# Last attention of a four-part transformer block: turned weights in two PSUM banks, ScalarE sharing their copy, pieces in the single bank, and the output bias as a row of the projection

## The chip, the cores and the metric

The kernel runs on one core of a Trainium2 chip. Its metric is the device time in microseconds of one execution; lower is better. Everything is float32. Beside the plain time of several runs there is one execution taken by the hardware profiler: each engine's instructions with start and duration. PE is the matrix engine (TensorE), DVE is VectorE, ACT is ScalarE, POOL is GpSimd, SP starts transfers. "PEclk" is the clock that the matrix engine was granted, 1.0 being full speed. PSUM, where matmuls write, has eight banks of 512 float32 values per partition here: `ps_s` holds three buffers of two banks, `ps_mm` is one bank, `ps_o` is one bank.

## The reference, cut to what matters

x has 8 sequences of 512 rows of 256 values. Four residual blocks follow one another: attention a, a feedforward block of two layers, attention b, and the same feedforward block again. The change touches attention b alone (16 heads of 16 values):

```
x = x + attn_a(layernorm(x)); x = x + ffn(layernorm(x))
x = x + attn_b(layernorm(x)); x = x + ffn(layernorm(x))
# attn_b
q, k, v   = split(x @ w_qkv + b_qkv, 3), by heads
dot       = einsum('bhid,bhjd->bhij', q, k)
scores    = dot*dot / (|q|^2 + |k|^2.T - 2.0*dot + 1e-6) + causal mask
out       = softmax(scores) @ v
return out @ w_out + b_out
```

## The kernel before, in words

The 8 sequences are taken in two groups of 4. For each group the program runs attention a, a feedforward block, attention b and a feedforward block, so there are two attention b stages, each over 4 sequences ("batches" in the code).

**A unit.** Attention b is cut into units: one block of 128 query rows, the key blocks up to the diagonal, and two or more heads. Row block 0 has 2 units of 8 heads x 128 keys, row block 1 has 4 units of 4 heads x 256, row block 2 has 8 units of 2 x 384, row block 3 has 8 units of 2 x 512. That is 22 units for a batch and 88 for a stage; all are 128 x 1024 in size, but those of row block 2, which are 128 x 768. For a unit, in the order of its data:

- PE computes the denominator (`den`) and the dot products (`dot`), each into a two-bank buffer of `ps_s` (L1079).
- ACT forms 1/den as exp(-ln(den)) (`inverse`, two instructions of L228); DVE repairs it by one Newton step: `error` (L1098, which reads `den` in PSUM) and `refine` (L1102).
- ACT squares `dot` into SBUF (`squares`, L1108); POOL adds the causal mask on the diagonal block (L1110).
- DVE multiplies by 1/den and takes the row maximum (`highest`, one instruction and one accumulator read a head, L1118); ACT takes the exponentials with their row sums (`exponentials`, L228, one a head).
- PE transposes the weights in 128 x 128 blocks (`turn`, L1148) and DVE copies them to SBUF (`keep_turned`, L1153). Before the change, the unit's two halves, 4 transposes each (3 in row block 2), go one after the other through the single bank `ps_mm`: transposes, copy, transposes, copy.
- PE multiplies them with the values into `ps_o` (`values`).

**A step.** The order of the work is written out by hand: `each_part(s)` issues a different stage of several units, one unit a step. Step s issues, on PE: `den` of unit s interleaved with `dot` of s-1, first half of `turn` of s-3, the first part of a piece, in odd steps the `values` of units s-5 and s-4, then the second half of `turn`, and the second part of the piece; on DVE: `refine` of s-1, `highest` of s-2, first `keep_turned`, `error` of s, second `keep_turned`, and the DVE part of a piece; on ACT: `inverse` of s, the ACT part of a piece, `squares` of s-1, `exponentials` of s-2. A helper (`order_keeper`) ties every instruction to the one issued before it on its engine, so this order is the order of execution. The engines themselves wait only for data and for buffers.

**Pieces.** In each step at most one "piece" of other work rides along. Projections of a finished row block are two pieces: `turned`, four transposes of the inverse sums (L1191), an ACT copy (L1195) and a DVE multiply (L1199); and `projected`, four matmuls (L1204) and the DVE addition to x (L1209). The prologue of the next batch is eleven: one that turns the normalized rows (8 transposes, L967, one ACT copy of 128x1024, L971); eight "side" pieces (`project` two matmuls L981, ACT square L991, the norm matmuls L994, DVE `keep_side` L1007), which are not placed in the steps with `values`; and two value pieces (matmuls L1024, DVE addition L1038). Before the change each of these takes one of the three buffers of `ps_s`. What is left of a prologue when its batch starts (each 22 steps) is run whole, piece after piece, with no other work in between.

**Norms.** Ahead of a prologue the rows of the next batch are normalized in the first two steps of the batch before it: statistics on DVE (and 1/std on POOL, L250 and L251), then the rows on DVE, and with them POOL adds the output bias to x in place (L953).

The steps of the prediction are to be followed in `each_part`, the loop under it, and the functions printed here:

Of the kernel before, what the change touches and what calls it, by code (L numbers as in the profile page):

```python
# [17 lines left out]
P = 128  # L18
# [26 lines left out]
def kernel(  # L45
# [152 lines left out]
    keep(near[:, 1, :], -1, NEG)  # L198
    causal = const.tile([P, P], F32, name="causal")
# [740 lines left out]
    def attention_b(batches, g):  # L940
        wl_b, wr_b, wv_b, wo_b, bv_b, bo_b = weights_b(g)

        def normalized(b):
# [6 lines left out]
            def rows():  # L950
                yr = pool.tile([P, NT, D], F32, tag="yr", name=f"yr_b{b}", bufs=1)
                normalize_rows([xs[b]], [yr], got["mv"], got["rstd"])
                nc.gpsimd.tensor_add(xs[b], xs[b], bo_b.unsqueeze(1).to_broadcast([P, NT, D]))  # L953
                state[b] = {"yr": yr}
# [3 lines left out]
        def stacks_and_values(b):  # L958
# [4 lines left out]
            def turned():  # L963
                got["pt"] = ps_s.tile([P, 2, NT, P], F32, tag="s", name=f"pyt_b{b}")
                for k in range(2):
                    for t in range(NT):
                        nc.tensor.transpose(got["pt"][:, k, t, :], state[b]["yr"][:, t, k * P : (k + 1) * P], ident)  # L967

            def columns():
                got["yT"] = pool.tile([P, 2, T], F32, tag="hT", name=f"yT_b{b}")  # L970
                nc.scalar.copy(got["yT"], got.pop("pt").rearrange("p k t c -> p k (t c)"))  # L971

            yield Piece(False, first=turned, act=columns)

            def side_piece(side, w, j):
                vec = vec_b[:, side, j, :]

                def project():
                    got["pu"] = ps_s.tile([P, 2, T], F32, tag="s", name=f"pu_b{b}_{side}_{j}")[:, 0]
# [38 lines left out]
            def value_piece(t2):  # L1018
                def project():
                    got["pv"] = ps_s.tile([P, 2, 2, HB * HDB], F32, tag="s", name=f"pv_b{b}_{t2}")  # L1020
                    for i in range(2):
                        t = 2 * t2 + i
                        for k in range(2):
                            nc.tensor.matmul(  # L1024
                                got["pv"][:, i, 0],
# [6 lines left out]
                def keep_values():  # L1032
# [4 lines left out]
                    for i in range(2):  # L1037
                        nc.vector.tensor_add(state[b]["v"][:, 2 * t2 + i, : HB * HDB], pv[:, i, 0], bv_b)  # L1038
# [21 lines left out]
        def unit(b, i, qp, js, first, last):  # L1060
# [84 lines left out]
            def turn(p, a):  # L1145
                ppt = ps_mm.tile([P, NT, P], F32, tag="mm", name=f"ppt_{n}_{a}")
                for k in range(cols // P):
                    nc.tensor.transpose(ppt[:, k, :], p[:, a, k * P : (k + 1) * P], ident)  # L1148
                return ppt

            def keep_turned(ppt, pt, a):
                nblocks = cols // P
                nc.vector.tensor_copy(pt[:, a, :nblocks, :], ppt[:, :nblocks, :])  # L1153
# [24 lines left out]
            def project(sums):  # L1178
# [9 lines left out]
                def turned():  # L1188
                    got["prt"] = ps_s.tile([P, 2, 4, P], F32, tag="s", name=f"prt_{n}")[:, 0]
# [11 lines left out]
                def projected():  # L1201
                    got["pp"] = ps_s.tile([P, 2, T], F32, tag="s", name=f"pp_{n}")[:, 0, :D]
                    for k in range(4):
                        nc.tensor.matmul(  # L1204
                            got["pp"], lhsT=got["oT"][:, k, :], rhs=wo_b[:, k, :], start=(k == 0), stop=(k == 3)
# [17 lines left out]
        def run(ahead):  # L1223
# [3 lines left out]

            tables_of(EXP_TABLES)
            each, count = len(units) // len(batches), len(units)
            den, dot, r, t, num, most, sums, ppt, pt = ({} for _ in range(9))  # L1230
# [16 lines left out]
            def each_part(s):  # L1247
# [24 lines left out]
                if unit_of(3):  # L1272
                    pt[s - 3] = pool.tile([P, 2, NT, P], F32, tag="pt", name=f"pt_{units[s - 3].n}", bufs=3)
                    turned = units[s - 3].turn(num[s - 3], 0)
# [7 lines left out]
                do(piece.act)  # L1282
                if unit_of(1):
                    num[s - 1] = units[s - 1].squares(dot.pop(s - 1))
                if unit_of(2):
                    most[s - 2] = units[s - 2].highest(num[s - 2], r.pop(s - 2))
                if unit_of(3):
                    units[s - 3].keep_turned(turned, pt[s - 3], 0)
                    turned = units[s - 3].turn(num.pop(s - 3), 1)
                do(piece.second)  # L1290
                if unit_of(2):
                    sums[s - 2] = units[s - 2].exponentials(num[s - 2], most.pop(s - 2))
                if unit_of(0):
                    t[s] = units[s].error(den.pop(s), r[s])
                if unit_of(3):
                    units[s - 3].keep_turned(turned, pt[s - 3], 1)
# [141 lines left out]
```

## Time and profile before

| what | us |
|---|---|
| three runs, median | 4909.79 |
| their lowest and highest | 4900.09 and 4925.63 |
| the profiled execution | 4923.95 |
| its span in the profile | 4922.2 |
| busy in the span: PE, DVE, ACT, POOL | 4458.2, 3161.6, 2244.1, 1276.0 |
| mean granted clock of PE | 0.945 |
| first attention b stage, about 1133 to 1697 | some 564 |
| second attention b stage, about 3584 to 4150 | some 566 |

The two stages are about 23% of the span; the change has no instruction in the rest. In each of them DVE is busy for 87% of the time and PE for 78%, at a mean clock of 0.79 to 0.87 in its parts, while over the whole span PE is busy for 91% and DVE for 64%. A group of instructions in the profile is one line of the kernel, one engine, one operation and one shape, with its busy time and the mean of one in ns; a wait is the idle time of an engine ahead of an instruction, with what ended it.

### The profile page before, as it was taken

To read this page: it belongs to the slowest core of one execution; us is meant where nothing else is said; L and a number is where in the kernel's file an instruction comes from. 1 tells how busy PE (TensorE), PEld (TensorE's weight loads), DVE (VectorE), ACT (ScalarE), POOL (GpSimd) and SP (SyncE) were. 2 spreads that over 40 slices of the span, in tenths; PEclk is the share of its full clock that TensorE was granted. 3 is DMA by queue.
4 is the path that set the end of the run, shared out by engine and by line. 5 is a ranking of instruction groups with operands and counts; after the bars stand their busy time and mean duration, and the time that the engine had idled before them with its cause. 6 is when DMAs were issued, how large, how long until landed. Compare 5 with 4: busy or idle time off the path is not lost. (4 is left out here: it accounts for less than half of the span.)

```text
span 4922.2 us, 68727 instructions
## 1 busy us (share of the span) xinstructions
PE 4458.2 (91%) x26240; PEld 2701.7 (55%) x26240; DVE 3161.6 (64%) x7400; ACT 2244.1 (46%) x5228; POOL 1276.0 (26%) x1164
## 2 busy tenths in 40 slices
PE   8999899898778898998999998998987778989989
PEld 5666556554444465565566665565544444655655
DVE  5667537627988776276356684376289987753762
ACT  3345325416777653154133452253177775532541
POOL 0024214312222243143100242142122222421431
PEclk9999899998888899999999998999988888999999
DMA  2000000000000000000100000000000000000000
GB/s 74 1 20 5 22 18 4 18 6 18 1 1 1 18 5 6 3 18 14 45 27 1 18 5 22 18 5 22 0 18 1 1 1 18 5 5 18 5 6 17
DMA packets 50922, 63.17 MB, mean 13 GB/s; under 512 B 6257, under 2 KB 45345, under 8 KB 50593
## 3 DMA queue, kind: packets, MB, share of 16 engines
q1 hardware_dynamic: 50592, 58.77, 3.7%
q8 instruction: 208, 3.41, 0.3%
q14 instruction: 122, 0.99, 0.1%
HBM read 46.19 MB, written 4.19 MB: 10 GB/s over the span
## 5 line engine op out<-in xcount | busy, mean ns | idle before, releaser
L1148 PE MATMUL ppt_b<-ident,num_b 128*128 128x128 f32 x1280 | 250.6, 320 | 192.2 <-DVE pt_b L1153 151.6
L1148 PEld LDWEIGHTS ppt_b<-ident,num_b 128*128 128x128 f32 x1280 | 156.8, 158 | 376.6 <-ACT num_b L228 126.3
L1110 POOL TENSOR_TENSOR num_b<-num_b,causal 128x256 f32<-128x256 f32 (+2 forms) x176 | 172.0, 977 | 709.2 <-ACT num_b L1108 539.0
L228 ACT ACTIVATE p_a<-s_a,nm_a 128x512 f32<-128x512 f32 x256 | 173.6, 683 | 304.2 <-DVE nm_a L381 304.2
L228 ACT ACTIVATE num_b<-num_b,most_b 128x512 f32<-128x512 f32 (+3 forms) x512 | 280.7, 553 | 44.9 <-DVE most_b L1128 41.9
L1118 DVE CUSTOM_DVE_ANT_0 num_b<-num_b,r_b 128x512 f32<-128x512 f32 (+3 forms) x512 | 259.8, 555 | 4.6 <-POOL num_b L1110 4.6
L1079 PE MATMUL den_b<-st_b,st_b 18*128 18x384 f32 (+3 forms) x1024 | 243.3, 529 | 7.5 <-DVE t_b L1098 5.1
L1153 DVE COPY pt_b<-ppt_b 128x512 f32<-128x512 f32 (+1 forms) x352 | 223.6, 635 | 35.5 <-PE ppt_b L1148 34.0
L228 ACT ACTIVATE r_b<-den_b 128x1024 f32<-128x1024 f32 (+1 forms) x176 | 166.3, 945 | 153.2 <-PE den_b L1079 101.6
L1079 PE MATMUL dot_b<-st_b,st_b 16*128 16x384 f32 (+3 forms) x1024 | 218.1, 531 | 1.4 <-ACT num_b L1108 0.9
L228 ACT ACTIVATE p_f0y<-p_f0y,nm_f0y,rn_f0y 128x256 f32<-128x256 f32 (+1 forms) x256 | 143.7, 563 | 162.0 <-DVE nm_f0y L614 149.0
L228 ACT ACTIVATE p_f1y<-p_f1y,nm_f1y,rn_f1y 128x256 f32<-128x256 f32 (+1 forms) x256 | 143.7, 564 | 161.7 <-DVE nm_f1y L614 148.7
L228 ACT ACTIVATE p_f1x<-p_f1x,nm_f1x,rn_f1x 128x256 f32<-128x256 f32 (+1 forms) x256 | 143.7, 564 | 155.3 <-DVE nm_f1x L614 142.3
L228 ACT ACTIVATE p_f0x<-p_f0x,nm_f0x,rn_f0x 128x256 f32<-128x256 f32 (+1 forms) x256 | 143.7, 564 | 155.4 <-DVE nm_f0x L614 142.4
L1098 DVE TENSOR_TENSOR t_b<-den_b,r_b 128x1024 f32<-128x1024 f32 (+1 forms) x176 | 196.8, 1118 | 10.6 <-ACT r_b L228 9.5
L1102 DVE SCALAR_TENSOR_TENSOR r_b<-t_b,r_b 128x1024 f32<-128x1024 f32 (+1 forms) x176 | 198.0, 1125 | 0.1
L381 DVE TENSOR_REDUCE nm_a<-s_a 128x2 f32<-128x1024 f32 x128 | 156.2, 1221 | 62.3 <-PE s_a L377 61.1
L228 ACT ACTIVATE r_b<-r_b 128x1024 f32<-128x1024 f32 (+1 forms) x176 | 172.4, 980 | 5.5
L1108 ACT ACTIVATE num_b<-dot_b 128x1024 f32<-128x1024 f32 (+1 forms) x176 | 164.7, 936 | 0.0
L394 PEld LDWEIGHTS ppt_a<-ident,p_a 128*128 128x128 f32 x1024 | 109.9, 141 | 97.9 <-ACT p_a L228 39.6
L849 PE MATMUL pu_g0x<-hT_g0x,wg_0x 128*128 128x512 f32 (+1 forms) x352 | 161.5, 607 | 0.0
L849 PE MATMUL pu_g1x<-hT_g1x,wg_1x 128*128 128x512 f32 (+1 forms) x352 | 161.2, 606 | 0.0
(349 smaller groups left out, 11123.0 us busy)
## 6 DMA issues: line engine op xcount, KB each, us to landing
x<-in_x SPq DMA_DIRECT2D x8, 512.0 KB
out<-x SPq DMA_DIRECT2D x8, 512.0 KB
wf_0x<-in_f_wqkv SPq DMA_DIRECT2D x2, 1536.0 KB
wf_0y<-in_f_wqkv SPq DMA_DIRECT2D x2, 1536.0 KB
wf_1x<-in_f_wqkv SPq DMA_DIRECT2D x2, 1536.0 KB
wf_1y<-in_f_wqkv SPq DMA_DIRECT2D x2, 1536.0 KB
wg_0x<-in_f_w SPq DMA_DIRECT2D x2, 1386.0 KB
wg_0y<-in_f_w SPq DMA_DIRECT2D x2, 1386.0 KB
```

Of the source, the lines that this page charges most:

```text
L228: i = nc.scalar.activation(out, in_, func, **more).ins
L381: nc.vector.tensor_reduce(nm, s, AX.X, ALU.max, negate=True)
L394: nc.tensor.transpose(ppt[:, odd, k, :], p[:, odd, k * P : (k + 1) * P], ident)
L849: nc.tensor.matmul(pu[: cols.stop - cols.start, c], lhsT=w1[:, k, cols], rhs=hT[:, k, :], start=(k == 0), stop=(k == 1),)
L1079: return nc.tensor.matmul(s[:, a, m * width : (m + 1) * width], lhsT=left[at, j, past:width], rhs=right[at, j, :width], start=True, stop=True,
L1098: nc.vector.tensor_mul(t[:, :, :cols], den[:, :, :cols], r[:, :, :cols])
L1102: nc.vector.scalar_tensor_tensor(r[:, :, :cols], t[:, :, :cols], 2.0, r[:, :, :cols], ALU.subtract, ALU.mult)
L1108: nc.scalar.activation(num[:, :, :cols], dot[:, :, :cols], AF.Square, scale=-0.5)
L1110: nc.gpsimd.tensor_add(own, own, causal.unsqueeze(1).unsqueeze(1).to_broadcast([P, 2, len(js), P]))
L1118: nc.vector.tensor_tensor_reduce(out=s4[:, a, m, :], in0=s4[:, a, m, :], in1=r4[:, a, m, :], scale=-1.0, scalar=LOWEST, op0=ALU.mult, op1= ...
L1148: nc.tensor.transpose(ppt[:, k, :], p[:, a, k * P : (k + 1) * P], ident)
L1153: nc.vector.tensor_copy(pt[:, a, :nblocks, :], ppt[:, :nblocks, :])
```

## The change

- `turn` writes both halves of a unit (8 transposes, 6 in row block 2) into one two-bank buffer of `ps_s`, all ahead of the piece. In even steps DVE copies the whole buffer with one instruction after `error`; in odd steps DVE copies the first half there, and ACT copies the second half after the exponentials.
- The pieces (`pyt`, `pu`, `pv`, `prt`, `pp`) take the single bank `ps_mm` in place of a buffer of `ps_s`. The piece that turns the normalized rows becomes two, of 4 transposes and an ACT copy of 128x512 each. The second part of a piece is issued ahead of `squares`.
- POOL's addition of the output bias (L953) goes. In its place a matmul of a single row of ones with the bias row opens the sum of each projection.
- The norms of the third and fourth batch move from steps 0 and 1 of the batch ahead to the two steps before that batch starts (20 and 21 of the batch before it); those of the second batch stay.

```diff
--- before.py
+++ after.py
@@ -196,6 +196,8 @@
     nc.gpsimd.memset(near, 0.0)
     keep(near[:, 0, :], 1, NEG)
     keep(near[:, 1, :], -1, NEG)
+    ones = const.tile([1, P], F32, name="ones")
+    nc.gpsimd.memset(ones, 1.0)
     causal = const.tile([P, P], F32, name="causal")
     nc.gpsimd.memset(causal, 0.0)
     keep(causal, -1, NEG_B)
@@ -950,7 +952,6 @@
             def rows():
                 yr = pool.tile([P, NT, D], F32, tag="yr", name=f"yr_b{b}", bufs=1)
                 normalize_rows([xs[b]], [yr], got["mv"], got["rstd"])
-                nc.gpsimd.tensor_add(xs[b], xs[b], bo_b.unsqueeze(1).to_broadcast([P, NT, D]))
                 state[b] = {"yr": yr}
 
             return [Piece(False, dve=statistics), Piece(False, dve=rows)]
@@ -960,23 +961,25 @@
 
             got = {}
 
-            def turned():
-                got["pt"] = ps_s.tile([P, 2, NT, P], F32, tag="s", name=f"pyt_b{b}")
-                for k in range(2):
-                    for t in range(NT):
-                        nc.tensor.transpose(got["pt"][:, k, t, :], state[b]["yr"][:, t, k * P : (k + 1) * P], ident)
-
-            def columns():
-                got["yT"] = pool.tile([P, 2, T], F32, tag="hT", name=f"yT_b{b}")
-                nc.scalar.copy(got["yT"], got.pop("pt").rearrange("p k t c -> p k (t c)"))
-
-            yield Piece(False, first=turned, act=columns)
+            def column_piece(k):
+                def turned():
+                    got["pt"] = transposed(ps_mm, halves_of(state[b]["yr"]), k, f"pyt_b{b}_{k}")
+
+                def columns():
+                    if k == 0:
+                        got["yT"] = pool.tile([P, 2, T], F32, tag="hT", name=f"yT_b{b}")
+                    nc.scalar.copy(got["yT"][:, k, :], got.pop("pt"))
+
+                return Piece(False, first=turned, act=columns)
+
+            for k in range(2):
+                yield column_piece(k)
 
             def side_piece(side, w, j):
                 vec = vec_b[:, side, j, :]
 
                 def project():
-                    got["pu"] = ps_s.tile([P, 2, T], F32, tag="s", name=f"pu_b{b}_{side}_{j}")[:, 0]
+                    got["pu"] = ps_mm.tile([P, T], F32, tag="mm", name=f"pu_b{b}_{side}_{j}")
                     for k in range(2):
                         nc.tensor.matmul(
                             got["pu"],
@@ -1017,12 +1020,12 @@
 
             def value_piece(t2):
                 def project():
-                    got["pv"] = ps_s.tile([P, 2, 2, HB * HDB], F32, tag="s", name=f"pv_b{b}_{t2}")
+                    got["pv"] = ps_mm.tile([P, 2, HB * HDB], F32, tag="mm", name=f"pv_b{b}_{t2}")
                     for i in range(2):
                         t = 2 * t2 + i
                         for k in range(2):
                             nc.tensor.matmul(
-                                got["pv"][:, i, 0],
+                                got["pv"][:, i],
                                 lhsT=got["yT"][:, k, t * P : (t + 1) * P],
                                 rhs=wv_b[:, k, :],
                                 start=(k == 0),
@@ -1035,7 +1038,7 @@
                         nc.gpsimd.memset(state[b]["v"][:, :, HB * HDB :], 0.0)
                     pv = got.pop("pv")
                     for i in range(2):
-                        nc.vector.tensor_add(state[b]["v"][:, 2 * t2 + i, : HB * HDB], pv[:, i, 0], bv_b)
+                        nc.vector.tensor_add(state[b]["v"][:, 2 * t2 + i, : HB * HDB], pv[:, i], bv_b)
 
                 return Piece(False, first=project, dve=keep_values)
 
@@ -1142,15 +1145,16 @@
                     )
                 return sums
 
-            def turn(p, a):
-                ppt = ps_mm.tile([P, NT, P], F32, tag="mm", name=f"ppt_{n}_{a}")
-                for k in range(cols // P):
-                    nc.tensor.transpose(ppt[:, k, :], p[:, a, k * P : (k + 1) * P], ident)
+            def turn(p):
+                ppt = ps_s.tile([P, 2, NT, P], F32, tag="s", name=f"ppt_{n}")
+                for a in range(2):
+                    for k in range(cols // P):
+                        nc.tensor.transpose(ppt[:, a, k, :], p[:, a, k * P : (k + 1) * P], ident)
                 return ppt
 
-            def keep_turned(ppt, pt, a):
+            def keep_turned(copy, ppt, pt, halves):
                 nblocks = cols // P
-                nc.vector.tensor_copy(pt[:, a, :nblocks, :], ppt[:, :nblocks, :])
+                copy(pt[:, halves, :nblocks, :], ppt[:, halves, :nblocks, :])
 
             def values(pt):
                 if first:
@@ -1186,7 +1190,7 @@
                 rows = rb.rearrange("p h d -> p (h d)")
 
                 def turned():
-                    got["prt"] = ps_s.tile([P, 2, 4, P], F32, tag="s", name=f"prt_{n}")[:, 0]
+                    got["prt"] = ps_mm.tile([P, 4, P], F32, tag="mm", name=f"prt_{n}")
                     for k in range(4):
                         nc.tensor.transpose(got["prt"][:, k, :], rows[:, k * P : (k + 1) * P], ident)
 
@@ -1199,10 +1203,11 @@
                     nc.vector.tensor_mul(got["oT"], state["o"], got.pop("rt"))
 
                 def projected():
-                    got["pp"] = ps_s.tile([P, 2, T], F32, tag="s", name=f"pp_{n}")[:, 0, :D]
+                    got["pp"] = ps_mm.tile([P, D], F32, tag="mm", name=f"pp_{n}")
+                    nc.tensor.matmul(got["pp"], lhsT=ones, rhs=bo_b[0:1, :], start=True, stop=False)
                     for k in range(4):
                         nc.tensor.matmul(
-                            got["pp"], lhsT=got["oT"][:, k, :], rhs=wo_b[:, k, :], start=(k == 0), stop=(k == 3)
+                            got["pp"], lhsT=got["oT"][:, k, :], rhs=wo_b[:, k, :], start=False, stop=(k == 3)
                         )
 
                 def added():
@@ -1225,9 +1230,10 @@
             tables_of(EXP_TABLES)
             each, count = len(units) // len(batches), len(units)
-            den, dot, r, t, num, most, sums, ppt, pt = ({} for _ in range(9))
+            den, dot, r, t, num, sums, pt = ({} for _ in range(7))
             kept_order = order_keeper()
             norms, prologues, projections = deque(), deque(), deque()
 
@@ -1271,7 +1277,7 @@
                     in_turns(*products)
                 if unit_of(3):
                     pt[s - 3] = pool.tile([P, 2, NT, P], F32, tag="pt", name=f"pt_{units[s - 3].n}", bufs=3)
-                    turned = units[s - 3].turn(num[s - 3], 0)
+                    turned = units[s - 3].turn(num.pop(s - 3))
                 do(piece.first)
                 if with_values:
                     in_turns(*[units[u].values(pt.pop(u)) for u in (s - 5, s - 4)])
@@ -1280,20 +1286,20 @@
                 if unit_of(0):
                     r[s] = units[s].inverse(den[s])
                 do(piece.act)
+                do(piece.second)
                 if unit_of(1):
                     num[s - 1] = units[s - 1].squares(dot.pop(s - 1))
                 if unit_of(2):
-                    most[s - 2] = units[s - 2].highest(num[s - 2], r.pop(s - 2))
-                if unit_of(3):
-                    units[s - 3].keep_turned(turned, pt[s - 3], 0)
-                    turned = units[s - 3].turn(num.pop(s - 3), 1)
-                do(piece.second)
-                if unit_of(2):
-                    sums[s - 2] = units[s - 2].exponentials(num[s - 2], most.pop(s - 2))
+                    most = units[s - 2].highest(num[s - 2], r.pop(s - 2))
+                    sums[s - 2] = units[s - 2].exponentials(num[s - 2], most)
                 if unit_of(0):
                     t[s] = units[s].error(den.pop(s), r[s])
                 if unit_of(3):
-                    units[s - 3].keep_turned(turned, pt[s - 3], 1)
+                    if s % 2 == 1:
+                        units[s - 3].keep_turned(nc.vector.tensor_copy, turned, pt[s - 3], slice(0, 1))
+                        units[s - 3].keep_turned(nc.scalar.copy, turned, pt[s - 3], slice(1, 2))
+                    else:
+                        units[s - 3].keep_turned(nc.vector.tensor_copy, turned, pt[s - 3], slice(0, 2))
                 do(piece.dve)
                 if norms:
                     do(norms.popleft().dve)
@@ -1305,8 +1311,11 @@
                             whole((norms or prologues).popleft())
                     following = step // each + 1
                     if following < len(batches):
-                        norms.extend(normalized(batches[following]))
+                        if following == 1:
+                            norms.extend(normalized(batches[1]))
                         prologues = deque(stacks_and_values(batches[following]))
+                elif step % each == each - 2 and step // each + 2 < len(batches):
+                    norms.extend(normalized(batches[step // each + 2]))
                 with kept_order():
                     each_part(step)
                 if step > count - 6:
```

## The prediction

> **What bounds the kernel now.** First the page: shares and clock of the span.
>
> ```profile
> PE 4458.2 (91%) x26240; PEld 2701.7 (55%) x26240; DVE 3161.6 (64%) x7400; ACT 2244.1 (46%) x5228; POOL 1276.0 (26%) x1164
> PEclk9999899998888899999999998999988888999999
> ```
>
> PE bounds most of the program, but the clock dips in two places, the attention b stages. A table of busy time by stretch (columns: length, PE, its weight loads, DVE, ACT, POOL, clock, DMA) shows why:
>
> ```profile
> 1133.00:1240.00 107.00, 82.13 (x622) 44.92 (x620) 97.78 (x223) 85.05 (x174) 28.77 (x25) 0.87 0.05 20
> 1240.00:1370.00 130.00, 103.22 (x847) 62.80 (x844) 119.73 (x273) 103.24 (x205) 33.16 (x30) 0.87 0.00 1
> 1370.00:1520.00 150.00, 115.87 (x913) 68.52 (x911) 133.39 (x306) 110.01 (x215) 36.22 (x36) 0.86 0.00 1
> ```
>
> DVE fills 89 to 92% of each; PE 77 to 79%, ACT 73 to 79%. So a stage goes at DVE's pace, with ACT close behind. The list of waits between 1150 and 1670 tells what DVE's gaps and the neighbours wait for:
>
> ```profile
> PE ppt_b L1148 <- DVE pt_b L1153: 67.5, 48, 5.6
> ACT r_b L228 <- PE den_b L1079: 34.3, 28, 5.9
> ACT sq_b L991 <- PE pu_b L981: 27.7, 18, 2.9
> DVE st_b L1007 <- PE pu_b L994: 25.6, 18, 2.8
> DVE pt_b L1153 <- PE ppt_b L1148: 14.8, 15, 2.5
> ```
>
> DVE itself waits little: 25.6 us for side pieces and 14.8 us for transposes. PE's 67.5 us behind L1153 are an echo of DVE's pace. Last the groups of the same stretch, with the shapes apart:
>
> ```profile
> L1153 DVE COPY pt_b<-ppt_b 128x512 f32<-128x512 f32 x106 | 72.5, 683 | 13.1 <-PE ppt_b L1148 12.4
> L1153 DVE COPY pt_b<-ppt_b 128x384 f32<-128x384 f32 x64 | 35.2, 550 | 2.4 <-PE ppt_b L1148 2.4
> L1195 ACT COPY rt_b<-prt_b 128x512 f32<-128x512 f32 x15 | 8.7, 578 | 1.9 <-PE prt_b L1191 1.6
> ```
>
> [...] the timeline (start, length) has
>
> ```profile
> 1275.85 3.48 POOL L953 TENSOR_TENSOR x<-x,wb 128x1024 f32<-128x1024 f32 x1 [1.52 <-PE den_b L1079]
> 1277.03 2.45 DVE L1118 CUSTOM_DVE_ANT_0 num_b<-num_b,r_b 128x128 f32<-128x128 f32 x1
> ```
>
> while the same instruction lasts 0.28 us beside it. [...]
>
> **The change, part by part,** per stage, in us; minus is gained.
>
> *Turned copies, DVE.* The step-to-step spacing of back-to-back copies in the timeline is some 0.08 below the duration: 0.60 for 512, 0.47 for 384. In the 44 odd steps one copy leaves DVE: 28 x 0.60 + 16 x 0.47 = -24.3. In the 44 even steps one 128x1024 replaces two; attention a's copy of that form takes 1215 ns, 1.13 spaced, against 1.20: 44 x 0.065 = -2.9. Together **-27.2**.
>
> *Bias add.* L953 ran four times a stage, three of them amid the steps, each stretching one L1118 by 2.45 - 0.28 = 2.17: **-6.5**. The second stretched L1118 in the same steps lies beside L1110 and stays. The row matmul: the four matmuls of a projection (eight records) take 1.89 at full clock, so at most 0.47 x 16 = 7.5 on PE, and nothing where PE's 22% idle hides it. I take 0; keep 7.5.
>
> *Turn waits.* DVE's 14.8 behind transposes: both halves now come long before the copy, which sits after `error`. But the eight transposes stand ahead of the piece and wait for a `ps_s` buffer, and what is queued behind them on PE is the piece and the values. I take **-5** of 14.8 (0 to -14).
>
> *ACT.* 28 x 0.48 + 16 x 0.38 = 19.5 (copies of 578 ns spaced, and the same less 128 elements) goes onto ACT in odd steps. ACT is busy 4.42 of a mean step of 6.09 (88 steps of one stage in the timeline), so an odd step hides it, unless ACT is behind. It is behind in steps with a side piece: its square waits for L981 (the 27.7 above), and L981 now stands behind eight transposes instead of four, 0.42 later. In row block 3 a pair of an odd step and an even side step takes ACT about 10.5 before and after, so the 0.67 that DVE saves there is lost: about 9 of the 16 side steps, **+5**. Two side pieces fall in steps with eight short exponentials (24 and 46), where ACT sums to about 14 over two steps against 12.0: **+4**.
>
> *Side pieces at a batch start.* Counting pieces through the steps, the split of the first piece and the later start leave 3, 3 and 2 side pieces for the batch starts, against 1, 3 and 3; so 16, not 17, ride in steps (**-1.5**). Run whole they now share one bank. Before, side pieces overlap in three buffers:
>
> ```profile
> 1388.04 1.88 PE L981 MATMUL pu_b<-yT_b,wb 128*128 128x512 f32 x4
> 1389.96 0.69 ACT L991 ACTIVATE sq_b<-pu_b,vec_b 128x512 f32<-128x512 f32 x1 [2.93 <-PE pu_b L981]
> 1390.70 1.13 PE L994 MATMUL pu_b<-sq_b,sel_b 128*128 128x512 f32 x2 [0.78 <-ACT sq_b L991]
> 1391.86 0.81 DVE L1007 TENSOR_SCALAR st_b<-pu_b,vec_b 128x512 f32<-128x512 f32 x1 [2.81 <-PE pu_b L994]
> ```
>
> The next L1007 follows the last (1388.24) by 3.62. In one bank the next L981 waits for L1007 too: 1.88 + 0.69 + 1.13 + 0.81 and hand-overs = 4.66. So 8 x 4.66 - 7 x 3.62 = **+12** at full clock. PE is then busy 3.0 of 4.66, 0.65; where that halves the clock, a piece takes 3.0 more, less the part overlapped: I put it at 7.2. I take that for one of the three starts: 8/3 x 2.5 = **+7** (0 to +20).
>
> *Rest.* DVE's copies in the drain of a stage's last five steps, -2; its start, where pieces run in one bank beside another stage whose PE is full, +1.5. The moved norms issue the same instructions on DVE and POOL two steps earlier, with no DMA; no queue of SP is touched: 0. Fewer PE gaps, more full clock: some 165 us of a stage pass at half clock now; **-4** (0 to -10).
>
> Sum: -27.2 - 6.5 - 5 + 5 + 4 - 1.5 + 12 + 7 - 2 + 1.5 - 4 = -17 a stage, -34 in both. The profiled execution, 4923.95, would become 4890; it stands 14 above the median of the runs, so the median becomes **4876**, -0.7%. What a measurement can tell here from no change is 0.5%, 25 us: below 4885 or above 4934.
>
> **The rivals.** *DVE's saving comes out whole.* For it: DVE is the busiest engine in every stretch, and the saved copies lie on it. Then ACT's losses (+9) and the half-clock start (+7) vanish and all the turn waits (-9 more) go: -42 a stage, -84: about 4826. Against it: ACT at up to 79% with an in-order queue.
>
> *ScalarE takes DVE's place.* In even steps DVE's copy waits for nothing new, but the next odd step's transposes wait for the ACT half behind the exponentials. If ACT sets most pairs, the 27.2 shrink to about 10: 0 a stage, about 4910. For it: its waits of 34.3 for `den` show ACT already late in the loop; against it: those are waits of ACT, so it has slack.
>
> *Slower: the single bank holds PE up.* A piece keeps the bank until its DVE part, the last of a step, and the next piece's matmuls stand on PE ahead of the values and of the next `den`. If each of the 16 side pieces in steps holds PE up by its L1007 and the 0.42 that L981 comes later (1.23), that is +20; and PE so interrupted runs the batch starts at half clock, all three (+13 more): +16 a stage, about 4942. It decides, after the +13, from 0.25 us a piece on (-17 + 13 + 16 x 0.25 = 0), and from 1.0 on by more than a measurement can miss. For it: PE's share of 0.65 at the batch starts, the 34.3 that ACT waits for `den`; against it: in most steps the bank is free well before the transposes end.
>
> **How the numbers follow.** My forecast 0.48 (own range 4855 to 4900, a good half of it below 4885), whole saving 0.24, ScalarE 0.12, slower 0.16. Faster: 0.28 + 0.24 = 0.52; slower 0.13 of the 0.16, since that case begins below its bound; same 0.35. The range leaves out a tenth at either side: 4815 to 4936.
>
> **What would show it.** Right: the 128x512 copies on DVE halve and come back on ACT at 0.58 us; no L1118 stretched by an addition to x; whole side pieces 4.6 to 7.2 us apart; L1153 without waits. Wrong: long waits of DVE behind ACT's `inverse`, PE waits behind ACT's copy, or a stage clock that falls below 0.8. Transfers cannot decide: DMA is at 0.00 to 0.05 of its share in these stretches.

## The result and the profile after

The changed kernel is slower: 4985.85 us median of 4 runs (4980.84 to 4990.49) against 4906.92 for the kernel before in the same comparison, a ratio of 1.0155, 95% interval 1.0124 to 1.0185. The prediction was 4876, with a range of 4815 to 4936. The profiled execution has a span of 4979.1 us against 4922.2, so 56.9 us are to be found.

The page of the changed kernel, its shares and clock, and then the busy time by stretch (columns as before: length, PE, weight loads, DVE, ACT, POOL, clock, DMA):

```profile
PE 4508.8 (91%) x26304; PEld 2733.7 (55%) x26304; DVE 3107.8 (62%) x7224; ACT 2276.1 (46%) x5324; POOL 1248.5 (25%) x1157
PEclk9999899998879899999999999999988788999999
```

```profile
1133.00:1240.00 107.00, 81.51 (x596) 47.74 (x598) 87.33 (x199) 81.77 (x173) 24.43 (x23) 0.84 0.06 21
1240.00:1370.00 130.00, 103.60 (x762) 61.48 (x756) 100.18 (x226) 93.66 (x195) 25.70 (x26) 0.87 0.00 1
1370.00:1520.00 150.00, 118.53 (x845) 69.31 (x844) 113.18 (x263) 102.35 (x210) 31.15 (x33) 0.81 0.00 1
```

DVE has become idle: 82, 77 and 75% of these stretches against 91, 92 and 89% before, and the third has lost clock (0.81 against 0.86). DVE's saving has come as idle time. Over the span it has 54 us less to do. What it waits for, and what the others wait for, in the list of waits from 1150 to 1690 (the wait in all, how often, the longest):

```profile
ACT sq_b L994 <- PE pu_b L984: 48.0, 21, 6.9
DVE st_b L1010 <- PE pu_b L997: 46.6, 21, 6.7
PE den_b L1082 <- ACT num_b L1111: 30.5, 27, 2.2
PE ppt_b L1152 <- ACT pt_b L1157: 24.1, 29, 2.4
DVE t_b L1101 <- ACT r_b L230: 23.2, 34, 1.6
DVE x L1214 <- PE pp_b L1209: 20.1, 9, 3.1
```

The wait of L1153 for transposes (14.8 before) is gone, as forecast. Five others have come: DVE's wait for side pieces has risen from 25.6 to 46.6; PE waits for ScalarE's copy; PE waits ahead of `den` for the squares; DVE's `error` waits for ScalarE's `inverse`; and DVE waits for the projections' matmuls. Of the third and fourth the list of the kernel before, for the same stretch, has only this (PEld is PE's loading of weights):

```profile
PEld den_b L1079 <- ACT num_b L1108: 0.8, 4, 0.3
DVE t_b L1098 <- ACT r_b L228: 2.2, 5, 0.6
```

Where the time lies is read best by steps. The timeline gives each step as the distance from one `error` (L1098 before, L1101 after) to the next; I add them by kind: the three steps that hold a batch start, nine around the norms (eight in which they run in one of the kernels, and the step at the same place of the third batch), the fifteen in which a projection is added to x, and the other sixty. The first stage, then the second, in us:

| kernel | starts | norms | projections | others | sum |
|---|---|---|---|---|---|
| before | 49.9, 49.9 | 73.0, 70.7 | 75.1, 75.1 | 332.1, 330.8 | 530.1, 526.5 |
| changed | 74.6, 75.0 | 60.9, 60.8 | 98.3, 106.9 | 335.5, 336.4 | 569.3, 579.1 |

Some 92 us are lost in the steps. About 13 a stage come back in the drain behind the last step (the first matmul of the next feedforward's scores is 16.2 us behind the last `error`, where it was 29.1), and 9 more between the stages. The losses lie in two places, the batch starts (+25 a stage) and the projection steps (+23 and +32). The norm steps gain 12 and 10. The sixty other steps are the riddle: DVE has its copies less, and they are 3 to 6 us longer.

The two places in the timeline (start, length, engine, line). First a batch start of the changed kernel:

```profile
1417.40 3.78 PE L984 MATMUL pu_b<-yT_b,wb 128*128 128x512 f32 x4 [0.97 <-DVE st_b L1010]
1421.22 0.69 ACT L994 ACTIVATE sq_b<-pu_b,vec_b 128x512 f32<-128x512 f32 x1 [5.97 <-PE pu_b L984]
1421.96 2.08 PE L997 MATMUL pu_b<-sq_b,sel_b 128*128 128x512 f32 x2 [0.78 <-ACT sq_b L994]
1424.08 0.81 DVE L1010 TENSOR_SCALAR st_b<-pu_b,vec_b 128x512 f32<-128x512 f32 x1 [5.79 <-PE pu_b L997]
```

One piece after the other, this L1010 7.53 behind the last (1416.55), and L984 at 3.78 where it took 1.88: half clock. At the other two starts of the stage the side pieces pass at full clock (1.00 granted from 1260 to 1276 and from 1560 to 1572), 4.79 apart. What sets this start apart stands just ahead of it:

```profile
1415.31 1.13 PE L997 MATMUL pu_b<-sq_b,sel_b 128*128 128x512 f32 x2 [3.69 <-ACT sq_b L994]
```

PE idled for 3.69 us, since ScalarE's square came late; ScalarE's exponentials had waited 3.46 us for DVE's row maximum, and DVE was at the moved norms and those of the next feedforward. The granted clock is 1.00 from 1409.72 to 1416.55, and 0.50 for the 23.9 us behind that, in which PE is busy for 79% of the time. The longest idle at the other two starts is 1.96 and 1.65 us.

Then a projection step:

```profile
1617.74 0.57 ACT L1157 COPY pt_b<-ppt_b 128x512 f32<-128x512 f32 x1
...
1618.36 1.97 PE L1152 MATMUL ppt_b<-ident,num_b 128*128 128x128 f32 x8 [1.00 <-ACT pt_b L1157]
...
1620.26 1.22 PE L1207 MATMUL pp_b<-wb,ones 1*128 1x256 f32 x2
...
1621.41 3.63 PE L1209 MATMUL pp_b<-wb,oT_b 128*128 128x256 f32 x8
...
1624.97 0.58 PE L1082 MATMUL den_b<-st_b,st_b 18*128 18x384 f32 x1
...
1625.08 0.42 DVE L1214 TENSOR_TENSOR x<-pp_b,x 128x256 f32<-128x256 f32 x1 [3.06 <-PE pp_b L1209]
...
1625.95 0.81 ACT L230 ACTIVATE r_b<-den_b 128x768 f32<-128x768 f32 x1 [3.18 <-PE dot_b L1082]
```

ScalarE's copy, behind its exponentials, ends at 1618.31; only then do the eight transposes begin, and behind them on PE stand the row matmul, the projection and the next `den`, all but `den` at half clock (0.50 granted from 1618 to about 1624.8). DVE waits 3.06 and ACT 3.18 for what PE brings. The step lasts 7.93; before it was 4.83.

### The profile page after: what moved, and what is told of

Its sections match the earlier page's. It is cut to its first block, busy times and chain, and to the rows that moved or that the text cites. A ratio compares the mean times of both kernels' runs of the same rounds, so it can differ in the third digit from the quotient of the medians.

```text
span 4979.1 us, 68790 instructions
## 1 busy us (share of the span) xinstructions
PE 4508.8 (91%) x26304; PEld 2733.7 (55%) x26304; DVE 3107.8 (62%) x7224; ACT 2276.1 (46%) x5324; POOL 1248.5 (25%) x1157
## 5 line engine op out<-in xcount | busy, mean ns | idle before, releaser
L1152 PE MATMUL ppt_b<-ident,num_b 128*128 128x128 f32 x1280 | 217.8, 320 | 66.2 <-ACT pt_b L1157 48.9
L1121 DVE CUSTOM_DVE_ANT_0 num_b<-num_b,r_b 128x512 f32<-128x512 f32 (+3 forms) x512 | 240.1, 516 | 0.0
L1101 DVE TENSOR_TENSOR t_b<-den_b,r_b 128x1024 f32<-128x1024 f32 (+1 forms) x176 | 198.4, 1127 | 61.0 <-ACT r_b L230 55.9
L1105 DVE SCALAR_TENSOR_TENSOR r_b<-t_b,r_b 128x1024 f32<-128x1024 f32 (+1 forms) x176 | 214.5, 1219 | 0.1
L1082 PEld LDWEIGHTS den_b<-st_b,st_b 18*128 18x128 f32 x1024 | 113.4, 211 | 162.4 <-ACT num_b L1111 72.2
L851 PE MATMUL pu_g0y<-hT_g0y,wg_0y 128*128 128x512 f32 (+1 forms) x352 | 160.7, 605 | 0.0
```

The costliest lines, as they stand in the source:

```text
L851: nc.tensor.matmul(pu[: cols.stop - cols.start, c], lhsT=w1[:, k, cols], rhs=hT[:, k, :], start=(k == 0), stop=(k == 1),)
L1082: return nc.tensor.matmul(s[:, a, m * width : (m + 1) * width], lhsT=left[at, j, past:width], rhs=right[at, j, :width], start=True, stop=True,
L1101: nc.vector.tensor_mul(t[:, :, :cols], den[:, :, :cols], r[:, :, :cols])
L1105: nc.vector.scalar_tensor_tensor(r[:, :, :cols], t[:, :, :cols], 2.0, r[:, :, :cols], ALU.subtract, ALU.mult)
L1121: nc.vector.tensor_tensor_reduce(out=s4[:, a, m, :], in0=s4[:, a, m, :], in1=r4[:, a, m, :], scale=-1.0, scalar=LOWEST, op0=ALU.mult, op1= ...
L1152: nc.tensor.transpose(ppt[:, a, k, :], p[:, a, k * P : (k + 1) * P], ident)
```

## The experiments

Four theories came out of this. T1: ScalarE's copy comes late, and with it the transposes and all that stands behind them. T2: the single bank makes the whole pieces at the batch starts go one after the other, in part at half clock. T3: the row matmul. T4, formed later: the ring of three two-bank buffers is now filled by each step. Every ratio is to the kernel before on the same chip, with its 95% interval.

**No copy on ScalarE.** In every step DVE copies the whole buffer:

```diff
-                    if s % 2 == 1:
-                        units[s - 3].keep_turned(nc.vector.tensor_copy, turned, pt[s - 3], slice(0, 1))
-                        units[s - 3].keep_turned(nc.scalar.copy, turned, pt[s - 3], slice(1, 2))
-                    else:
-                        units[s - 3].keep_turned(nc.vector.tensor_copy, turned, pt[s - 3], slice(0, 2))
+                    units[s - 3].keep_turned(nc.vector.tensor_copy, turned, pt[s - 3], slice(0, 2))
```

> The changed kernel with DVE copying the whole turned buffer in every step, ScalarE none. Theory T1, ScalarE's late copy: in even steps the transposes, and behind them on PE the piece and the next den, wait for a copy that ScalarE makes after its exponentials (24 us of PE idle in the first stage); without it about 4950 or less, although DVE gets back some 22 us a stage. Theory T2, the single bank, or T3, the row matmul, alone: DVE's copies come on top, about 5000 to 5030.

4942.76, ratio 1.0046 (1.0031 to 1.0061): 1.1%, some 54 us, better than the changed kernel, though DVE has its copies again. The projection steps are back at 78.0 and 79.0, the starts still at 68.5 and 72.4. T1 holds, and it is not all.

**Pieces back in the two-bank buffers.** `pu`, `pv`, `prt` and `pp` as before:

```diff
-                    got["pu"] = ps_mm.tile([P, T], F32, tag="mm", name=f"pu_b{b}_{side}_{j}")
+                    got["pu"] = ps_s.tile([P, 2, T], F32, tag="s", name=f"pu_b{b}_{side}_{j}")[:, 0]
...
```

> The changed kernel with the pieces pu, pv, prt and pp back in the two-bank buffers (the turned rows of the next batch stay in the single bank). T2, the single bank: whole side pieces at the batch starts overlap again, 3.6 us apart and not 7.5, which gives back some 50 us over both stages: 4920 to 4940. T1: the same pieces now also wait in the ring of three buffers behind ScalarE's copy; 4980 to 5030.

5249.46, ratio 1.0674 (1.0658 to 1.0690), far beyond both. With the two-bank turn a step already takes all three buffers, and a piece becomes a fourth tenant: DVE waits 101.8 us for side pieces in the window 1150 to 1750. Its time says nothing on T2, though its starts fall to 54.6 and 54.5, as T2 would have it. It explains why the pieces went to the single bank, and it pointed at the ring.

**Bias on POOL again,** no row matmul:

```diff
+                nc.gpsimd.tensor_add(xs[b], xs[b], bo_b.unsqueeze(1).to_broadcast([P, NT, D]))
...
-                    nc.tensor.matmul(got["pp"], lhsT=ones, rhs=bo_b[0:1, :], start=True, stop=False)
```

> The changed kernel with the output bias added by POOL as before and no row matmul. T3, the row matmul: it takes 14 us of PE in the first stage, in steps that have become 23 us longer; without it 4940 to 4960, the stretched maximum (13 us) being paid again. T1 and T2: within 15 of the changed kernel, 4970 to 5000.

4960.67, ratio 1.0086 (1.0071 to 1.0101): some 34 us better than the changed kernel, at the edge of what T3 expected. The projection steps fall to 81.8 and 81.8, from 98.3 and 106.9.

**Norms in their old place.**

```diff
-                        if following == 1:
-                            norms.extend(normalized(batches[1]))
+                        norms.extend(normalized(batches[following]))
...
-                elif step % each == each - 2 and step // each + 2 < len(batches):
-                    norms.extend(normalized(batches[step // each + 2]))
```

> The changed kernel with the norms of every next batch in the first two steps of a batch, as before. If the norms' new place costs, 4960 or less; if it gains, as the shorter first steps in the profile suggest (some 6 us a stage beside what the bias add gave), 4985 to 5010.

5007.73, ratio 1.0176 (1.0159 to 1.0193). Its interval overlaps the changed kernel's; inconclusive, except that the moved norms are not where the loss comes from. The starts do become shorter, 66.3 and 70.7: the idle of 3.69 us at the middle one is 1.65 in the first stage, the clock stays full, and that start takes 23.2 us in place of 31.9. The projection and the other steps take more than that back.

**ScalarE's copy ahead of the exponentials.**

```diff
+                if unit_of(3) and s % 2 == 1:
+                    units[s - 3].keep_turned(nc.scalar.copy, turned, pt[s - 3], slice(1, 2))
                 if unit_of(2):
                     most = units[s - 2].highest(num[s - 2], r.pop(s - 2))
...
-                        units[s - 3].keep_turned(nc.scalar.copy, turned, pt[s - 3], slice(1, 2))
```

> The changed kernel with ScalarE's copy in odd steps moved from behind the exponentials to ahead of them. Theory T1 in the form 'the copy is late': the buffer comes free some 2 us earlier and the next transposes do not wait; at or below the kernel in which DVE copies all, 4910 to 4945. T1 in the form 'ScalarE has no time for it': no gain, the exponentials and the next ln are later instead, 4970 to 5000.

4948.33, ratio 1.0058 (1.0037 to 1.0079), like the kernel without the copy and 3 us above what T1 expected. ScalarE does the same work, and PE's wait behind L1157 (24.1) is no more in the list. So what these 48 us hung on was where the copy stood, not ScalarE's load.

**Whole pieces in the two-bank buffers,** all others in the single bank:

```diff
+        def piece_bank(name):
+            if between:
+                return ps_s.tile([P, 2, T], F32, tag="s", name=name)[:, 0]
+            return ps_mm.tile([P, T], F32, tag="mm", name=name)
...
+                        between.append(step)
                         while prologues or norms:
                             whole((norms or prologues).popleft())
+                        between.clear()
```

> The changed kernel, but the pieces that are run whole at a batch start take the two-bank buffers; all pieces inside steps stay in the single bank. T2, the single bank serializes the whole pieces at half clock: they come 3.6 us apart again, some 11 us at each of two starts and a little at the third, 45 to 50 us over both stages: 4940 to 4955. If the half clock there has another cause, 7 us apart at least: 4975 to 4995.

4947.77, ratio 1.0057 (1.0036 to 1.0079), 48 us better, within what T2 expected. The starts fall to 53.4 and 53.3. In its timeline the second of two whole pieces follows by 3.62 again, at full clock:

```profile
1408.58 0.81 DVE L1017 TENSOR_SCALAR st_b<-pu_b,vec_b 128x512 f32<-128x512 f32 x1 [3.39 <-PE pu_b L1004]
1412.20 0.81 DVE L1017 TENSOR_SCALAR st_b<-pu_b,vec_b 128x512 f32<-128x512 f32 x1 [2.81 <-PE pu_b L1004]
```

In this start PE idles ahead of its first L1004 as long as in the changed kernel, 3.64 us, and the clock halves behind it too, but for 3.4 us only, in which PE is busy for 3.33. So the clock halved at this start with either buffer; with the single bank, which leaves PE six gaps of 0.78 to 0.97 us there, it stayed at half for 23.9 us in place of 3.4. That it lasted because of the gaps is my estimate from these two stretches.

**No ScalarE copy and no row,** both edits from above:

> The changed kernel with no ScalarE copy (DVE copies all) and the bias added by POOL, no row matmul. If T1 and T3 are two separate costs, 54 + 34 us less than the changed kernel: about 4905. If both are the same delay of PE in the projection steps, about 4935 to 4945, no better than without the ScalarE copy alone.

4940.2, ratio 1.0043 (1.0029 to 1.0058): no better than without the copy alone. So T1 and T3 are, as far as their times tell, one delay: the row costs much only where PE is late already.

**The row alone, in the kernel before.**

```diff
-                nc.gpsimd.tensor_add(xs[b], xs[b], bo_b.unsqueeze(1).to_broadcast([P, NT, D]))
...
+                    nc.tensor.matmul(got["pp"], lhsT=ones, rhs=bo_b[0:1, :], start=True, stop=False)
```

> The kernel before with the row matmul in place of POOL's addition, and nothing else. T3 as a cost of the instruction wherever it stands: 32 rows of 1.2 us less the 13 us of stretched maxima, +25: about 4940. If the row costs only because PE sets the pace of those steps in the changed kernel: the 13 us are gained, about 4905.

4891.19, ratio 0.9944 (0.9927 to 0.9961), 28 us faster than before; beyond the better of the two expectations. In the norm steps 12.8 and 10.7 us a stage are gained, in the projection steps 5.7 and 2.5 lost. Its longest L1118 (here L1119) is 1.77 us, where before five in each stage had about 2.4:

```profile
L1119 DVE CUSTOM_DVE_ANT_0 num_b<-num_b,r_b x512: 276/548/1766, 1142.5 to 4094.6; 128x128 f32<-128x128 f32 x43, 128x384 f32<-128x384 f32 x43, 128x512 f32<-128x512 f32 x43, 128x256 f32<-128x256 f32 x42
```

(Instruction and operands, then shortest, median and longest in ns.)

**Early copy and whole pieces apart,** both edits from above:

> The changed kernel with both of its two costs taken away: ScalarE's copy ahead of the exponentials, and whole pieces at the batch starts in the two-bank buffers. If late copy (48 us) and single bank at the starts (48 us) are separate, their sum: about 0.996 of the kernel before, 4900. If they are one delay counted twice: about 4940. If nothing else costs, the DVE time saved should show too and it should lie below the kernel before with row and moved norms (below 4880).

4914.69, ratio 0.9999 (0.9990 to 1.0007), between the 4900 of the sum and the 4940 of one delay. The two gains of 0.97 and 0.98% come to 1.56%, four fifths of their sum, so they are two costs that overlap a little. But with row and 27 us a stage of DVE less, it is only level with the kernel before, so something else takes them. Projections are at 85.0 and 85.4 and the other steps at 333.8 and 332.3, no shorter than before. A step in it, from the timeline:

```profile
1494.25 1.00 ACT L1118 ACTIVATE num_b<-dot_b 128x1024 f32<-128x1024 f32 x1
...
1495.31 0.69 PE L1089 MATMUL den_b<-st_b,st_b 18*128 18x512 f32 x1 [1.53 <-ACT num_b L1118]
...
1497.02 1.02 ACT L230 ACTIVATE r_b<-den_b 128x1024 f32<-128x1024 f32 x1 [0.19 <-PE den_b L1089]
```

`den` stands still for 1.53 us until the squares have read `dot`, and starts 0.06 behind them. A step takes three two-bank buffers now, for `den`, `dot` and `ppt`, and there are three. So `den` has to wait for a buffer that the step just before has used. ln, exp, squares, `den`, ln is a closed loop without DVE in it.

ScalarE's load is a rival that this does not exclude. In the step shown ScalarE idles only 0.19 us ahead of the ln, since its copy and exponentials fill the time. Over the sixty other steps of the first stage it is busy for 292 of 334 us, DVE for 283; before it was 281 and DVE 304 of 332. In those stretches between two `error`s that begin in an odd step, and so hold its copies, ScalarE is busy for 96% (87% before). No run separates its load from the ring in this kernel.

**The kernel before with row and moved norms,** so the change without banks and turn:

> The kernel before with the row matmul and the moved norms: the change without the two-bank turn and without the pieces in the single bank. Row 28 us, norms 10 (the changed kernel lost 10 without them): about 4880. If the moved norms gain only because the changed kernel's batch starts are long: 4890, as with the row alone.

4886.28, ratio 0.9944 (0.9927 to 0.9961): the same as the row alone. The moved norms are worth nothing that can be measured here. With its interval wholly below 1 it is, beside the row alone, the version that beats both kernels.

**The same, with a half copied by ScalarE.** In odd steps the first half, ahead of the exponentials:

```diff
-                    units[s - 3].keep_turned(turned, pt[s - 3], 0)
+                    units[s - 3].keep_turned(turned, pt[s - 3], 0, nc.scalar.copy if s % 2 else nc.vector.tensor_copy)
```

> The same, and in odd steps ScalarE makes the first half's copy, ahead of its exponentials; turn, banks and pieces as before the change. DVE loses 24 us a stage; its copy of the first half lies behind the row maxima now, so the bank also comes free earlier for the second half. If DVE sets the pace: 35 to 50 us below the kernel without it, about 4840. If ScalarE or PE's clock takes its place: within 10 of it, about 4880.

4979.9, ratio 1.0130 (1.0110 to 1.0150), a plain miss: 94 us more than without, for 24 us a stage taken from DVE. Its list of waits, 1150 to 1690:

```profile
DVE pt_b L1154 <- PE ppt_b L1149: 61.6, 58, 4.1
PE ppt_b L1149 <- ACT pt_b L1154: 55.7, 42, 2.2
```

ScalarE reaches the copy only behind ln, exp and squares. With one bank for both halves, the second half's transposes wait for it, and DVE waits for them. T1 again, in the other kernel.

**The ring alone, in the kernel with row and moved norms.** A step without a piece takes a third buffer behind `error`:

```diff
+                if not piece.first and s < count:
+                    hold = ps_s.tile([P, 2, T], F32, tag="s", name=f"hold_{units[0].n}_{s}")
+                    nc.vector.memset(hold[0:1, 0, 0:1], 0.0)
                 do(piece.dve)
```

> The kernel before with row and moved norms, and one more thing: in every step without a piece a third two-bank buffer is taken behind error (DVE writes one element of it), so that each step takes all three buffers as the two-bank turn does. Theory T4, the ring: den and dot now get the buffers that the step before has just used and wait for its square or error; the 28 us that lie between the repaired changed kernel and this one's base come back, or more, since DVE has its copies too: 4910 to 4960. Rival, the single bank inside the steps: the ring costs nothing and this stays at 4880 to 4895.

4934.64, ratio 1.0041 (1.0026 to 1.0055), 48 us more than its base, as T4 expected; the memsets themselves are 2.2 us of DVE in the first stage (38 of 59 ns). The sixty other steps go from 325.7 and 330.0 to 350.1 and 346.8; the starts and projection steps of the first stage give 10 back, and some 16 us of the loss lie outside the steps. So filling the ring costs the sixty steps 24 and 17 us, most of what the copies save a stage. The list of waits does not show it as plainly as in the changed kernel: `den` and its weight loads wait only some 5 us for the squares there, and from 1150 to 1660 the clock falls from 0.91 to 0.87. By which wait the ring acts in this kernel is open. The rival, that the single bank holds PE up inside the steps, has nothing for it in the changed kernel's trace either: in the first stage PE waits for that bank ahead of a piece only at the three batch starts and once at the stage's own beginning.

**Squares ahead of ln and exp,** to free the buffer sooner, in the changed kernel with early copy and whole pieces apart:

```diff
+                if unit_of(1):
+                    num[s - 1] = units[s - 1].squares(dot.pop(s - 1))
                 if unit_of(0):
                     r[s] = units[s].inverse(den[s])
...
-                if unit_of(1):
-                    num[s - 1] = units[s - 1].squares(dot.pop(s - 1))
```

> The changed kernel with early ScalarE copy and two-bank buffers at the batch starts, and on ScalarE the squares ahead of ln and exp, so that the buffer of dot, which the next den takes, comes free 2 us earlier. T4: the wait of den for the squares (30 us of PE in the first stage) goes and a part of DVE's saving shows: 4870 to 4900. Rival: ln and exp come 1 us later and error waits for them instead: 4910 to 4940.

4986.26, ratio 1.0145 (1.0128 to 1.0162), slower than both expectations and 1.46% more than without this edit. The wait has not gone but moved; its list of waits, 1150 to 1690:

```profile
ACT num_b L1118 <- PE dot_b L1089: 66.7, 62, 3.6
PE dot_b L1089 <- DVE t_b L1108: 46.4, 40, 2.8
DVE t_b L1108 <- ACT r_b L230: 36.9, 37, 2.6
```

Now `dot` waits for `error` to have read `den`, and `error` for an exp that comes 1 us later. Whichever of the two reads is put first, the other holds the third buffer.

## Why the prediction was wrong

The sum came to -17 us a stage; the steps lost 39 and 53. What failed is that DVE's saving was carried over in full to the stage, while PE's wait behind ScalarE's late copy (48 us in both stages) was put at nothing and the ring of buffers had no line at all. The batch starts, 25 a stage for the 19 forecast, were undersized.

*Turned copies, DVE: right.* Counted up to the start of the next instruction, the copies take 68.8 us of the first stage's steps in place of 95.2, so -26.4 for the -27.2 forecast. All of DVE's busy time there fell by 26.0, from 5.46 to 5.16 us in a mean step: L1118 takes 9.7 less, and `refine` 8.8 more, of which the last section tells. The new copies last what was said:

```profile
L1157 DVE COPY pt_b<-ppt_b 128x1024 f32<-128x1024 f32 x25 | 30.4, 1215 | 0.0
L1157 DVE COPY pt_b<-ppt_b 128x512 f32<-128x512 f32 x26 | 17.7, 680 | 0.0
```

What failed is the step from DVE's busy time to the stage's time. "So a stage goes at DVE's pace" holds only as long as no loop through the other engines is as long; the sixty other steps show none of the saving.

*The missing step: the ring.* The working had no line for the buffers of `den` and `dot`, though the turn's move into `ps_s` was in it. Before, a step drew two or three of the three buffers and `den` waited 0.8 us for squares; after, PE alone waited 30.5. With the ring alone worth 48 us in the other kernel, it is of the size of the two costs that the runs took out. Its size inside the changed kernel was not measured by itself, and there ScalarE's load stands beside it.

*Turn waits, -5: right for DVE, wrong for PE.* DVE's 14.8 went; another wait, of `error` for `inverse`, rose from 2.2 to 23.2. The clause "wait for a `ps_s` buffer, and what is queued behind them on PE is the piece and the values" named the mechanism and priced it at nothing. It is T1: 48 us in both stages by the early copy. This wait of PE and that of `error` are among the signs of being wrong that the prediction named.

*ACT, +9: wrong in kind.* It asked whether ScalarE has the time in odd steps, and took it as busy for 4.42 us of a mean step; the first stage's steps before the change have it busy for 406.8 of 530.1 us, 4.68 a step. With the same copies made earlier 48 us of the loss are gone, so for these the question was when the copy comes, and who stands behind it. Whether its time costs something beside that, the 96% above leave open.

*Bias add, -6.5 and 0 for the row: half right.* The removal was undersized: 12.8 and 10.7 us a stage in the norm steps of the kernel with the row alone. The second stretched L1118, which "lies beside L1110 and stays", went too; in the changed kernel one a stage has stayed (2.42 us at 1149.19). The row was hidden in the kernel before, with a small loss in the projection steps, but not in the changed one, where its step stands behind late transposes (34 us).

*Batch starts, +12 and +7: the one bank and the side pieces right, the cause of the half clock not, a term left out.* A side piece takes 4.79 at full clock for the 4.66 worked out and 7.53 at half clock for the 7.2. That half clock would come at one start of three was an estimate that came true, but PE's share does not show as its cause: at the other two starts the side pieces ran at a granted clock of 1.00 with PE busy for 3.10 of 4.79 us, 0.65. At the middle start the clock fell to 0.50 at 1416.55, behind PE's idle of 3.69 us, which the working has not, and 1.13 us of work. It fell behind the 3.64 us with whole pieces in the two-bank buffers too, and stayed full behind the 1.65 us with the norms in their old place. But at the last start it fell as well, at 1573.56 for 3.4 us, with no idle above 1.65 us ahead of it; what halved it there is not shown. Left out were the value pieces, which take the same bank: DVE waits 17.4 us for the six of the first stage, 2.08 to 3.87 each, against 5.7 before. These 11.7 us carry the starts to +24.7; all else there came to 13 of the 19 forecast.

*Rest.* The drain gave back 13 a stage, for the 2 forecast. The moved norms, put at 0, lie at the middle start now and have their part in its idle, but no gain or loss of the whole by them is clear of the noise. "Fewer PE gaps, more full clock", -4, an estimate, came out the other way: the clock is 0.84, 0.87 and 0.81 in the three stretches, where it was 0.87, 0.87 and 0.86.

*The rivals.* The slower one had the right sign, and its bank at the batch starts is shown, but with one start at half clock and not all three, and it is by far not the whole. Its other half, side pieces in steps that hold PE up for 1.23 each, is not in the trace: PE waits for L1010 ahead of a side piece five times in the first stage, 4.6 us in all, each time at a batch start. ScalarE in DVE's place was right that the next transposes wait for the ACT half, but gave it no loss beyond DVE's saving; moving the copy removed that loss.

## What to carry to other kernels

An engine at 90% is the bound only as far as no loop through other engines is nearly as long; before work is moved off it, follow the loop that the new buffers close. When a ring of buffers goes from partly to wholly used in each step, a producer can come to wait for the reader of just now (here 0.8 us of waiting became 30.5), and that belongs into the sum like an instruction does. A copy handed to another in-order engine is to be judged by when it comes there, not by whether that engine has time on average (here 48 us hung on its place).

## What the hardware showed that was not expected

In the changed kernel `refine` (L1105 after, L1102 before) falls together with POOL's mask additions more often. Thirteen of its instructions in both stages last over 1.6 us; before there were two.

```profile
1450.51 2.35 POOL L1113 TENSOR_TENSOR num_b<-num_b,causal 128x1024 f32<-128x1024 f32 x1 [4.22 <-ACT num_b L1111]
1450.67 3.27 DVE L1105 SCALAR_TENSOR_TENSOR r_b<-t_b,r_b 128x1024 f32<-128x1024 f32 x1
```

This one began 0.16 behind POOL's and ended 1.08 after it, about its own undisturbed length (1.22) counted from POOL's end at 1452.86. All thirteen are alike: they begin 0.16 to 0.72 us behind a mask addition of POOL and end 1.07 to 1.09 us behind its end. In the kernel before, a `refine` (1275.69) that began 0.16 ahead of POOL's addition to x, of the same 128x1024, took 1.22 us. So some 0.3 us in when `refine` begins against POOL lie between a stall and none; my estimate from these two cases is that a shift of that size on DVE can make or remove such stalls, without any of these instructions being edited. In the first stage `refine` takes 8.8 us more of DVE.
